# Stage 1 of a triangle update: four chunks batched singly, and a shift row asked for one step after its store

## Chip, cores, metric

The kernel runs on one core of one Trainium2 chip. The metric is the device time of one execution in microseconds; a median of three runs is given. A profile comes from one further execution of the same program, which has its own time.

## What is computed

The input x is 384 x 384 positions of 128 channels, all fp32. Two layers follow each other:

```
# layer 0
z     = layernorm(x)
left  = (z @ Wl + bl) * sigmoid(z @ Wlg + blg)
right = (z @ Wr + br) * sigmoid(z @ Wrg + brg)
core  = einsum('bikh,bjkh->bijh', left, right)
x     = x + sigmoid(x @ Wg + bg) * (layernorm(core) @ Wout + bout)
# layer 1
left  = x @ (W_left + W_eq) + biases
out   = left * sum_j(x @ W_right + b_right) * sigmoid(x @ W_gate + b_gate)
x     = layernorm(out @ W_out + b_out + x)
```

## The kernel before, in words

**Three stages.** Stage 1 (to about 1000 us) makes `left` and `right` and stores them in DRAM as `lr_d`. Stage 2 (to about 1700 us) makes `core` for one channel h after another, 18 fp32 matmul passes each. Stage 3 does the rest row by row. The change touches stage 1 alone.

**Stage 1's unit.** A chunk n is 8 x 128 positions of x; there are 144. A chunk is worked off in two steps, so step k = 2n + q, with q = 0 or 1; a step is two halves of two 128x512 matmuls (`back`, L362: matmul L372 into a PSUM tile `pr`, of which there are three; sigmoid on ScalarE L383; gating on VectorE L385, which writes the tile `lr`). Each fp32 matmul is recorded as two passes, so a step is 8 passes.

**The layer norm.** For z, the matmul needs x minus its mean, with the reciprocal root of the variance applied afterwards as a scale. VectorE takes the statistics of each position from `xt` (L263). Statistics are finished in batches of chunks: `powers` (L265, VectorE, L275 to L279) makes moments, `power` (L282, GpSimd, L286) raises to the power -0.5, once for 8 columns, at most once a step, and `centres` (L292, VectorE, L303 and L304) makes the shift `nd`. `begin` (L451) starts a batch when its statistics are there and fewer than two batches are under way; it is called once a step, as is `centres`.

**How the shift reaches the data.** The first 8 chunks are loaded with positions in partitions, shifted there (L320) and transposed on TensorE (L335, by `front`). From chunk 8 on, the chunk is loaded a second time with channels in partitions (`load_columns`, L129, tile `xc`, four buffers). Its shift must then lie along the free dimension, in all partitions alike. So `store_nd` (L346) writes the batch's `nd` to DRAM, in pieces of 16 bytes; `load_shift` (L136, DMA on L139) reads one row of 512 values into partition 0 of a tile `bc` (four buffers), for each step one row; and `shift` (L314) broadcasts it over the partitions on GpSimd (L323) and subtracts it from the columns (L324). From step 10 on, step k of the program holds the shift for step k + 2.

**What sets the order.** The order on every engine is that of the program. All DMAs of the stage are issued by SyncE in order, so a DMA whose wait isn't fulfilled holds up all that follow. In each step the loop at L459 issues, in this order: a store of shifts that has become due (L348), the columns of chunk n + 4 (L134, in the second step of a chunk), rows of shifts (L139), chunks for the statistics (L127), one slice of 1 MB of a finished `lr` tile (L357, `store_slice`). A tile `lr` holds 8 chunks; its 8 slices go out in the steps after its last chunk, so for the first tile in steps 15 to 22.

**The batches.** Chunks 0 to 9 are batches of one, then come (10, 11), (12, 13) and so on in pairs. **When a row is asked for:** L501 looks at the first row that is still wanted. It is asked for when it is at most 6 steps ahead, and its store lies in an earlier step; if it is more than 3 steps ahead, the store must lie at least two steps back.

Of the kernel before, what the change touches and what calls it, by code (L numbers as in the profile page):

```python
# [19 lines left out]
def triangle_then_gated_row_kernel(ctx: ExitStack, tc: tile.TileContext, a: dict, out: bass.AP):  # L20
# [35 lines left out]
    def seq(ins):  # L56

        return tc.keep_in_program_order(ins)
# [4 lines left out]
    def load(dst, src, queue=nc.sync):  # L63
        seq(queue.dma_start(out=dst, in_=src))
# [12 lines left out]
    chunks = [(kb, ig, c) for kb in range(NB) for ig in range(NG) for c in range(G // XR)]  # L77
    kept = {(NB - 1, ig): None for ig in range(NG - KEEP, NG)}
    end2 = ctx.enter_context(ExitStack())
    with ExitStack() as ctx2:  # L80
# [16 lines left out]
        with tc.tile_pool(name="p1w", bufs=5, side="right") as wp, \  # L97
# [6 lines left out]
            NQ = XR // 4  # L104
            AHEAD, LEAD = 4, 15
            FETCH = 6
# [1 line left out]
            loaded, normed = {}, {}  # L108
            lr, full = {}, []
            batches, at = [(n, n + 1) for n in range(PLAIN)], PLAIN  # L110
            for size in [1, 1] + [2] * len(chunks):
                if at < len(chunks):
                    batches.append((at, min(at + size, len(chunks))))
                    at = batches[-1][1]
# [167 lines left out]
            def power():  # L282

                own, lo, hi, span = pows.pop(0)
                sd, rs = (t[:, lo:hi] for t in terms[own][2:])
                seq(nc.gpsimd.tensor_tensor(rs, sd, mhalf[:, :hi - lo], ALU.pow))  # L286
                if hi == span[1]:
                    means.append((own, span))
                    if 0 < own[0] < PLAIN:
                        centres(1)  # L290
# [16 lines left out]
            centred, stored = [], {}  # L307
# [6 lines left out]
            def shift(n, q, rows=slice(0, 4)):  # L314


                s = slice(4 * q + rows.start, 4 * q + rows.stop)
                if n < PLAIN:
                    nd = nds[n, n + 1][:, s].unsqueeze(2).to_broadcast([P, rows.stop - rows.start, C])
                    seq(nc.gpsimd.tensor_tensor(loaded[n][:, s], loaded[n][:, s], nd, ALU.subtract))  # L320
                else:
                    z, t = columns[n][:, q].rearrange("c k i -> c (k i)"), shifts.pop((n, q))
                    seq(nc.gpsimd.partition_broadcast(t, t[0:1]))  # L323
                    seq(nc.gpsimd.tensor_tensor(z, z, t, ALU.subtract))  # L324

            def front(n, q, rows=slice(0, 4)):

                if n < PLAIN:  # L330
                    s = slice(4 * q + rows.start, 4 * q + rows.stop)
                    columns[n] = loaded[n]
                    pt = tps.tile([P, 4, P], F32, tag="pt", name="pt")
                    for r in range(s.start, s.stop):
                        seq(nc.tensor.transpose(pt[:, r - s.start, :], loaded[n][:, r, :], ident))  # L335
                    seq(nc.scalar.copy(columns[n][:, s], pt[:, :s.stop - s.start]))
# [25 lines left out]
            def back(n, q, half, between=None):  # L362


                kb, ig, c = chunks[n]
                if c == 0 and q == 0 and half == 0:
                    lr[kb, ig] = lrp.tile([P, H, G, 2], F32, tag="lr", name="lr")
                t = lr[kb, ig]
                pr = pps.tile([P, 2, 4 * H], F32, tag="pr", name="pr")
                for r in range(2):  # L370
                    i = 2 * half + r
                    seq(nc.tensor.matmul(  # L372
                        pr[:, r, :], lhsT=columns[n][:, 4 * q + i, :] if n < PLAIN else columns[n][:, q, :, i],
                        rhs=wz, start=True, stop=True,
                    ))
                    if r == 0 and between:
                        between()
                r0 = 4 * q + 2 * half
                own, c0 = normed[n]
                rs = [terms[own][3][:, c0 + r:c0 + r + 1] for r in range(r0, r0 + 2)]  # L380
                sg = [wp.tile([P, 2 * H], F32, tag="sg", name="sg") for _ in range(2)]
                for r in range(2):
                    seq(nc.scalar.activation(sg[r], pr[:, r, 2 * H:], AF.Sigmoid, scale=rs[r]))  # L383
                for r in range(2):
                    seq(nc.vector.scalar_tensor_tensor(  # L385
                        t[:, :, c * XR + r0 + r, :],
                        pr[:, r, :2 * H].rearrange("k (h s) -> k h s", s=2),
                        rs[r],
                        sg[r].rearrange("k (h s) -> k h s", s=2),
                        ALU.mult, ALU.mult,  # L390
                    ))
                if c == G // XR - 1 and q == NQ - 1 and half == 1:
                    if (kb, ig) in kept:
                        kept[kb, ig] = t
                    else:
                        full.extend((kb, ig, hs, t) for hs in range(0, H, HS))
# [40 lines left out]
            want = [i for i, (n, q) in enumerate(steps) if n >= PLAIN]  # L437

            def goal(k):

                if k < 0:
                    return 2 * AHEAD
                return 2 * (k + 1) + min(2 * LEAD, 10 + (10 * k + 6) // 7 if k < 8 else 20 + 2 * (k - 7) // 3)

            for n in range(PLAIN, len(chunks)):
                k = 2 + (n - PLAIN) // 2
# [4 lines left out]
            def begin(k):  # L451

                while waiting and 2 * NQ * waiting[0][1] <= given and (k == 0 or free()):
                    own = waiting.pop(0)
                    powers(own, 0, XR * (own[1] - own[0]))
                    if k > 0:
                        break

            for k, (n, q) in enumerate(steps):  # L459
                early = len(means)  # L460
                for _ in range(min(len(pows), 1)):
                    power()
                early = 0 if k in (6, 7, 8) else early if k > 8 else len(means)
                if k > 0:
                    more = 4 if k in (6, len(steps) - 6) else 1
                    while shifted < min(len(steps), k + 2 + more):
                        shift(*steps[shifted])
                        shifted += 1
                    if more > 1:
                        lib = library_config.all_libraries[10] if k == 6 else library_config.standard  # L470
                        seq(nc.gpsimd.load_library(lib))
                for half in range(2):
                    if k == 0:

                        back(n, q, half, (lambda: front(*steps[1])) if half else None)
                        if half == 0:
                            centres(len(means))
                            shift(*steps[2])
                            shifted = 3
                    else:  # L480
                        back(n, q, half)
                        if half == 0:
                            centres(early)
                        if half == 0 and k + 1 < len(steps):
                            front(*steps[k + 1])
                    if half == 0 and k > 0:
                        begin(k)
                    stats_to((goal(k - 1) + goal(k)) // 2 if half == 0 else goal(k))
                if k == 0:
                    begin(k)  # L490
                    power()
                if q == NQ - 1:
                    del loaded[n], normed[n], columns[n]
                while centred:
                    own = centred.pop(0)
                    if own[0] >= PLAIN:
                        store_nd(own)
                        stored.update({m: k for m in range(*own)})
                if q == NQ - 1:
                    load_columns(n + 4)  # L500
                while want and want[0] <= k + FETCH and stored.get(want[0] // NQ, k) < k - (want[0] > k + 3):  # L501
                    load_shift(*steps[want.pop(0)])
                assert not want or want[0] > k + 3
                for m in fetch.get(k, []):
                    load_chunk(m)
                store_slice()
                if k == 4:
                    for t, src in later:
                        load(t, src)
                if k == 20:  # L510
                    m2 = late_weights()
                if k == 24:
                    late_products(m2)
                if k == len(steps) - 2 * G // 4 + 16:
                    assert not full
                    for h in range(2):
                        load_h(h)
# [465 lines left out]
```

## Time and profile before

| | |
|---|---|
| median of 3 runs | 3162.54 us (3160.98 to 3163.11) |
| the profiled execution: its time | 3165.75 us |
| its span, first to last instruction | 3163.6 us |
| TensorE busy | 3138.1 us (99%) |
| VectorE, ScalarE, GpSimd busy | 2471.1, 1805.8, 2396.2 us |
| L372, stage 1's matmul on `xc` | 2176 passes, 937.6 us |
| L357, L127, L134: one transfer | 1024, 512, 512 KB |
| L348, store of a pair or of one chunk; L139, one row | 8 or 4 KB; 2 KB |

A timeline line is: start in us, duration, engine, line, operation, tiles, count; in brackets the idle time before it and what ended that. `PE` is TensorE, `DVE` VectorE, `ACT` ScalarE, `POOL` GpSimd, `SPq` SyncE's issue of a DMA (not its transfer). A line of a window gives, after its length, the busy time of TensorE, its weight loads, VectorE, ScalarE and GpSimd, then the granted TensorE clock, the share of the DMA engines, and GB/s. When a DMA lands is read from the updates of its semaphore, which the trace also holds.

### The profile page before, as it was taken

How to read it: one execution, taken by the hardware profiler on the slowest of the kernel's cores; microseconds unless marked ns; L12 is line 12 of the kernel's file. 1: busy time of each engine (PE TensorE's matmuls, PEld its weight loads, DVE VectorE, ACT ScalarE, POOL GpSimd, SP SyncE). 2: the span in 40 equal slices, each digit the busy share in tenths (PEclk: the TensorE clock that was granted, in tenths of full speed). 3: DMA queues.
4: the chain of work that ended last, by engine and by line, in shares of the span. 5: the costliest groups of instructions: out<-in, count | busy, mean ns of one | idle time of the engine just before them, and what ended most of it. 6: DMA issues, size and time to landing. Idle time of an engine off the chain costs nothing.

```text
span 3163.6 us, 44516 instructions
## 1 busy us (share of the span) xinstructions
PE 3138.1 (99%) x11306; PEld 2133.0 (67%) x11306; DVE 2471.1 (78%) x7395; ACT 1805.8 (57%) x3755; POOL 2396.2 (76%) x3066
## 2 busy tenths in 40 slices
PE   9999999999999999999999999999999999999998
PEld 4677777777776666666666566677777777777776
DVE  8788888888886555555555788888888888888998
ACT  4444444444444334334343577677777777777776
POOL 6788888888886665666666587788888888888887
PEclk9999999999999999999999999999999999999999
DMA  4887878888883999999999865666666666666562
GB/s 163 290 327 276 341 281 323 292 318 309 295 326 96 281 283 284 284 281 284 282 282 284 287 239 198 225 223 220 220 220 220 220 220 220 220 220 220 210 211 109
DMA packets 509070, 797.42 MB, mean 252 GB/s; under 512 B 56657, under 2 KB 419537, under 8 KB 492434
## 3 DMA queue, kind: packets, MB, share of 16 engines
q1 hardware_dynamic: 507520, 792.61, 73.8%
q8 instruction: 94, 1.54, 0.2%
q10 hardware_dynamic: 1234, 1.77, 0.2%
q14 instruction: 158, 1.29, 0.1%
q0 software_dynamic: 64, 0.20, 0.0%
HBM read 508.14 MB, written 286.36 MB: 251 GB/s over the span
## 4 chain that ended last, share of the span: by engine, by line
PE 97%; DVE 1%; DMA 0%; issue 0%; POOL 0%; ACT 0%; SPq 0%; POOLq 0%; DVEq 0%; ACTq 0%
PE pr L372 30%; PE pc L611 23%; PE py L781 8%; PE pr L752 8%; PE pg L769 8%; PE pl L770 8%; PE pg L721 8%; PE py L782 4%; DMA core_d<-ct 0%; DVE lr L385 0%; POOL rs L286 0%; PE pq L729 0%; DVE st L263 0%; PE pt L335 0%; DMA stage<-in_x_nat_dram 0%
## 5 line engine op out<-in xcount | busy, mean ns | idle before, releaser
L372 PE MATMUL pr<-wz,xc 128*128 128x512 f32 x2176 | 937.6, 594 | 5.7 <-POOL xc L324 4.6
L372 PEld LDWEIGHTS pr<-wz,xc 128*128 128x128 f32 x2176 | 670.6, 308 | 272.0 <-issue 5.4
L383 ACT ACTIVATE sg<-pr,rs 128x256 f32<-128x256 f32 x1152 | 482.7, 470 | 517.6 <-ACT sg L383 354.6
L611 PE MATMUL pc<-rr,lrh 128*128 128x384 f32 x2304 | 743.3, 486 | 0.4 <-DVE lr L385 0.4
L611 PEld LDWEIGHTS pc<-rr,lrh 128*128 128x128 f32 x2304 | 452.0, 196 | 291.8 <-issue 1.1
L385 DVE SCALAR_TENSOR_TENSOR lr<-pr,rs,sg 128x256 f32<-128x256 f32 x1152 | 502.6, 478 | 174.8 <-ACT sg L383 169.4
L816 ACT ACTIVATE py<-py,nm,rs 128x128 f32<-128x128 f32 x1149 | 491.9, 429 | 158.7 <-DVE u L774 80.1
L781 PEld LDWEIGHTS py<-wo,u 128*128 128x128 f32 x2304 | 376.6, 191 | 97.5
L622 DVE TENSOR_TENSOR csum<-csum,ct 128x1152 f32<-128x1152 f32 x127 | 175.4, 1381 | 333.7 <-ACT ct L620 333.7
L781 PE MATMUL py<-wo,u 128*128 128x128 f32 x2304 | 402.0, 275 | 0.0
L620 ACT COPY ct<-pc 128x1152 f32<-128x1152 f32 x127 | 142.2, 1119 | 445.3 <-PE pc L611 439.7
L743 POOL TENSOR_TENSOR cs<-ct,rt 128x384 f32<-128x384 f32 x380 | 378.7, 998 | 8.3 <-PE pg L769 4.2
L851 POOL TENSOR_TENSOR yt<-yt,lnb 128x384 f32<-128x384 f32 x380 | 379.7, 1001 | 2.9 <-DVE yt L845 2.6
L324 POOL TENSOR_TENSOR xc<-xc,bc 128x512 f32<-128x512 f32 x272 | 345.8, 1271 | 24.0
L286 POOL TENSOR_TENSOR rs<-nd,mhalf 128x8 f32<-128x8 f32 (+1 forms) x145 | 236.3, 1630 | 145.7 <-ACT sg L383 112.7
L796 DVE BATCH_NORM_STATS2 st<-py 128x6 f32<-128x128 f32 x1152 | 266.4, 287 | 88.7 <-PE py L782 86.7
L592 POOL COPY rr<-lrh 128x768 f32<-128x768 f32 x128 | 196.4, 1534 | 161.0 <-DMA lrh<-lr_d 150.3
L782 PE MATMUL py<-ident,x1T 128*128 128x128 f32 x1152 | 314.0, 273 | 0.0
L752 PE MATMUL pr<-cs,wc 128*128 128x384 f32 x768 | 313.5, 490 | 0.0
L721 PE MATMUL pg<-xt,mat_L_conv_Wg 128*128 128x384 f32 x768 | 310.7, 487 | 2.0 <-ACT ct L635 2.0
L769 PE MATMUL pg<-x1T,mat_L_conv_W_gate 128*128 128x384 f32 x768 | 310.7, 486 | 0.9 <-ACT g L772 0.9
L770 PE MATMUL pl<-x1T,mat_L_conv_W_left 128*128 128x384 f32 x768 | 310.5, 486 | 0.0
(124 smaller groups left out, 4297.0 us busy)
## 6 DMA issues: line engine op xcount, KB each, us to landing
lr_d<-lr SPq DMA_DIRECT2D x128, 1024.0 KB
lrh<-lr_d SPq DMA_DIRECT2D x128, 640.0 KB
xt<-in_x_row_dram SPq DMA_DIRECT2D x96, 768.0 KB
ct<-core_d SPq DMA_DIRECT2D x95, 768.0 KB
rt<-rstd_d SPq DMA_DIRECT2D x95, 768.0 KB
out_dram<-yt SPq DMA_DIRECT2D x94, 768.0 KB
core_d<-ct SPq DMA_DIRECT2D x125, 576.0 KB
xt<-in_x_nat_dram SPq DMA_DIRECT2D x136, 512.0 KB
```

The source lines that it names most:

```text
L372: seq(nc.tensor.matmul(pr[:, r, :], lhsT=columns[n][:, 4 * q + i, :] if n < PLAIN else columns[n][:, q, :, i], rhs=wz, start=True, stop=Tr ...
L383: seq(nc.scalar.activation(sg[r], pr[:, r, 2 * H:], AF.Sigmoid, scale=rs[r]))
L385: seq(nc.vector.scalar_tensor_tensor(t[:, :, c * XR + r0 + r, :], pr[:, r, :2 * H].rearrange("k (h s) -> k h s", s=2), rs[r], sg[r].rearra ...
L611: seq(nc.tensor.matmul(banks[ib], lhsT=t[:, kb, ib * P:(ib + 1) * P, 0], rhs=rr[:, kb], start=(kb == 0), stop=(kb == NB - 1),))
L721: seq(nc.tensor.matmul(pg[:, :N], lhsT=wg0, rhs=r["xT"], start=True, stop=True))
L752: seq(nc.tensor.matmul(pr[:, :N], lhsT=wc, rhs=r["cs"], start=True, stop=True))
L769: seq(nc.tensor.matmul(pg2[:, :N], lhsT=wgate, rhs=r["x1T"], start=True, stop=True))
L770: seq(nc.tensor.matmul(pl[:, :N], lhsT=wleft, rhs=r["x1T"], start=True, stop=True))
L781: seq(nc.tensor.matmul(py[:, s], lhsT=r["u"][:, s], rhs=r["wo"], start=True, stop=False))
L782: seq(nc.tensor.matmul(py[:, s], lhsT=r["x1T"][:, s], rhs=ident, start=False, stop=True, is_transpose=True))
L816: seq(nc.scalar.activation(py[:, s], py[:, s], AF.Identity, bias=bias, scale=scale))
L851: seq(engine.tensor_tensor(yt, yt, lnbb, ALU.add))
```

## The change

Two lines. The list of batch sizes after the first 8 chunks begins with six ones in place of two, so chunks 10, 11, 12 and 13 are batches of their own, and pairs begin with (14, 15). And a row may be asked for in the step after the step of its store, however far ahead it is wanted.

```diff
-            for size in [1, 1] + [2] * len(chunks):
+            for size in [1] * 6 + [2] * len(chunks):
...
-                while want and want[0] <= k + FETCH and stored.get(want[0] // NQ, k) < k - (want[0] > k + 3):
+                while want and want[0] <= k + FETCH and stored.get(want[0] // NQ, k) < k:
                     load_shift(*steps[want.pop(0)])
```

The order of the program around it becomes, step by step (S: store of a batch's shifts, R: row asked for):

| step | before | after |
|---|---|---|
| 11 | | R 8,0 and 8,1 |
| 12 | S 9; R 8,0 and 8,1 | S 9 |
| 13 | | S 10; R 9,0 and 9,1 |
| 14 | R 9,0 and 9,1 | R 10,0 |
| 15 | | S 11; R 10,1 |
| 16 | S 10-11 | S 12; R 11,0 |
| 17 | R 10,0 | R 11,1 |
| 18 | R 10,1, 11,0 and 11,1 | S 13; R 12,0 |
| 19 | S 12-13 | R 12,1 |
| 20 | | R 13,0 |
| 21 | R 12,0, 12,1, 13,0 and 13,1 | R 13,1 |
| 22 | S 14-15 | S 14-15 |
| 23 | | R 14,0 and 14,1 |
| 24 | R 14,0, 14,1 and 15,0 | R 15,0 |
| 26, 27 | in 27: R 16,0 and 16,1 | in 26: R 16,0; in 27: R 16,1 |

From step 28 on both are alike. On VectorE the moments of 10-11 (step 13) and 12-13 (step 16) become those of 10, 11, 12 and 13 (steps 11, 13, 14, 16), their `centres` those of steps 13, 15, 16 and 18 in place of 16 and 19. On GpSimd the powers of steps 14, 15, 17 and 18 become those of steps 12, 14, 15 and 17. Instructions of other kinds are neither added nor moved.

## Prediction

> **What bounds the kernel now.** I read the page's chain of waits first, then TensorE's waits, then the stretch in which it waits, engine by engine. The unit below is the step k = (n, q) of stage 1: half a chunk n, 8 matmul passes (each fp32 matmul is recorded as two). T(k) is the time at which its first pass starts; "row (n,q)" is the 2 KB shift row that L139 fetches for it.
>
> ```profile
> span 3163.6 us, 44516 instructions
> ...
> PE 97%; DVE 1%; DMA 0%; issue 0%; POOL 0%; ACT 0%; SPq 0%; POOLq 0%; DVEq 0%; ACTq 0%
> ```
> TensorE's own work is 97% of the chain, so only time in which it stands still or runs slowly can be won. Its waits over the whole run are short; the first two lines are:
>
> ```profile
> PE pr L372 <- POOL xc L324: 4.6, 1, 4.6
> PE pr L372 <- ACT sg L383: 2.0, 2, 1.1
> ```
> One wait of 4.6 us on GpSimd's subtraction. The timeline places it, and the windows give the clock around it:
>
> ```profile
> 73.86 13.90 PE L372 MATMUL pr<-wz,xc 128*128 128x512 f32 x32
> 92.37 16.60 PE L372 MATMUL pr<-wz,xc 128*128 128x512 f32 x32 [4.62 <-POOL xc L324]
> 110.07 3.79 PE L372 MATMUL pr<-wz,xc 128*128 128x512 f32 x8 [1.10 <-ACT sg L383]
> ```
> ```profile
> 87.75:92.37 4.62, 0.01 (x1) 0.00 (x0) 3.04 (x16) 0.84 (x2) 2.05 (x2) 0.82 1.03 427
> 92.37:99.57 7.20, 7.20 (x11) 3.72 (x12) 1.27 (x4) 1.68 (x4) 6.66 (x6) 0.64 1.04 369
> 99.57:110.07 10.50, 9.41 (x22) 6.17 (x22) 10.40 (x33) 5.03 (x12) 6.16 (x6) 1.00 0.88 317
> ```
> 32 passes are four steps, k = 16 to 19, in 13.76 us: 3.44 us a step. The next four took 16.60, because after the standstill the granted clock is 0.64 (third number from the end) and 11 passes need 7.20 us. Then 1.10 us more are lost. Unhindered, T(24) would be 73.86 + 8 x 3.44 = 101.38; it is 110.07. **8.7 us** are at stake: 4.7 standstill, 2.9 slow clock, 1.1 second wait. From 114.9 us on TensorE doesn't pause again in this stage.
>
> Who is late? GpSimd, for a row, and SyncE's queue says why:
>
> ```profile
> 82.47 1.63 POOL L286 TENSOR_TENSOR rs<-nd,mhalf 128x8 f32<-128x8 f32 x1
> 90.18 0.80 POOL L323 PARTITION_BROADCAST bc<-bc  x1 [6.08 <-DMA bc<-nd_d]
> 91.06 1.26 POOL L324 TENSOR_TENSOR xc<-xc,bc 128x512 f32<-128x512 f32 x1
> ```
> ```profile
> 77.90 1.42 SPq L348 DMA_DIRECT2D nd_d<-nd  x1
> 80.63 0.33 SPq L127 DMA_DIRECT2D xt<-in_x_nat_dram  x1
> 81.01 0.45 SPq L357 DMA_DIRECT2D lr_d<-lr  x1
> 84.96 0.24 SPq L139 DMA_DIRECT2D bc<-nd_d  x1
> ```
> Shifts of chunks 10 and 11 are stored together at 77.90 (step 16). By the trace's completion events the store lands at 84.94, behind a 512 KB load and the first 1 MB slice of lr_d; row (10,0) is asked for at 84.96 and lands at 90.09, behind two more large transfers. Two trips through a full queue; TensorE starts 2.28 us after the row has landed (broadcast, subtraction, hand-over).
>
> **The skill.** "TensorE: Matmul & The Clock Gate", What's actually happening: an idle window of about 3.4 us puts the clock to half. The trace agrees: 4.62 us idle gave 0.64 over the next 7.2 us, 1.10 us idle left 1.00. "DMA: Bandwidth & Descriptors", Queues, rings and completion order: every engine consumes a ring's descriptors in order. It agrees: a 2 KB row took 1.3 us at 63.3 us, 5.1 us at 84.96. "SBUF — State Buffer", SBUF: two separate sides: a VectorE operation with two SBUF inputs and a GpSimd operation block each other. It agrees: L232 on 128x1 took 1.25 us under an L324, L279 1.23 us under another, 0.19 us elsewhere.
>
> **The change, part by part.** Replaying the step loop by hand gives each queue's order; from step 28 on both programs are the same.
>
> 1. *Row (10,0).* Chunk 10 is a batch of its own: moments in step 11, power in 12, store in 13 (about 66.8 us), row asked for in step 14, once its buffer is free (four rows, so after the shift of (8,0), which ends at 71.1). The DMAs are nearly idle then; it lands near 73. GpSimd reaches this shift at about 82.3 and ends it at 84.4; TensorE wants it at T(20) = 87.6. The 4.62 us wait and its slow clock go.
>
> 2. *VectorE and GpSimd.* Four single batches replace two pairs: 14 more VectorE instructions, 2 x (0.7 + 0.3) = 2 us in steps 11 to 18, where it waits 0.45 to 0.9 us for ScalarE in most half steps. One batch's moments (step 14, about 70.2) fall under the L324 of 69.8 to 71.1: up to 0.9 us; the next L385 would be 0.65 late against over 0.8 of slack in PSUM buffers. Cost 0. GpSimd does as many powers; the one put before the shift of (7,0) ends that shift near 62, needed at 64.4. Cost 0. Without these covers: up to 2 us.
>
> 3. *SyncE.* Two more stores (0.38 us of issue each), and the load of columns 11 moves behind a store, from 70.4 to about 74.8, wanted at 90: hidden, but its 0.5 MB now start the congested stretch; I add 0.3 us to what lands later. Rows (11,0) to (13,1) land between about 85 and 107; the tightest, (13,0), stored at 84.8, landed at 92.7, asked for at once, lands near 103.8 against a limit of 107.
>
> 4. *VectorE after step 20.* L227 to L234 still fall there (1.7 us in before) and 22's moments follow. This is what ended in the 1.10 us wait at T(24), with two operations stretched by GpSimd. GpSimd is ahead now and idle at step 22's moments. Bounds 0 and 1.1; I take 0.4.
>
> 5. *What is late next: row (14,0).* TensorE now runs 8.7 us earlier, but the eight lr_d slices (8 MB, steps 15 to 22) take the DMAs as long as before. In before the queue was never empty from 77 to 105; slice 6 landed at 104.89, columns 14 at 106.15. That stays. Between 84.77 and 106.15, 8 MB landed: 2.67 us per MB (2.4 for the quickest slices). Behind columns 14 come chunk 22 (0.5 MB), slice 7, the store of (14,15), chunk 23, slice 8, columns 15. An issue also waits for the eighth before it (eight semaphores in turn), so that store goes out at about 100. It lands 1.5 x 2.67 + 0.1 after 106.15: 110.3. Only then is row (14,0) asked for, now in step 23, and it stands behind 2 MB that are already queued: 110.3 + 5.1 = 115.4 (+0.3 of item 3 and -0.3 as a row rides on one ring and often lands ahead of the load before it). T(28) unhindered is 101.38 + 15.13 (as before's steps 24 to 28, L240 to L243 included) + 0.4 = 116.9. With the row it is 115.4 + 2.28 = 117.7: **0.8 us** of wait. Row (14,1) follows behind a power: its shift ends 1.64 + 2.13 = 3.8 us after the first, a step is 3.44: 0.3 more. Bounds: landing at 113.8 costs nothing, at 117.5 it costs 3.3.
>
> Sum: 8.7 - 0.4 - 0.8 - 0.3 = **7.2 us** less. All that follows is TensorE-bound and shifts as a whole. The profiled run took 3165.75 us (span 3163.6): 3158.6. Median shown 3162.54: **3155.3**.
>
> **Rivals.**
> - *No new wait*: the queue drains at 2.4 us per MB and row (14,0) lands by 114. For: slices 2, 3, 5 and 6 came at 2.4 to 2.5. Against: slices 1 and 4 took 4.2 and 3.5. Gain 8.7 - 0.4 = 8.3: 3154.2.
> - *The wait at step 28 is large*: the row lands at 117.5 and more. T(29) is then 117.5 + 6.0 = 123.5 instead of before's 128.6: gain 5.1, and if the standstill passes the idle window, 2.9 less. For: store-to-row trips of 7 us each way occur throughout 77 to 106. 3157.4 to 3160.3, middle 3158.5.
> - *Slower*: the same place, worse. If both trips of row (14,0) take 11.3 us, the longest latency in the stretch (slice 6), it lands at 100.1 + 22.6 = 122.7; T(29) = 122.7 + 6.0 + 2.9 for the clock = 131.6, against 128.6: 3.0 slower, 3165.5. It decides from a landing of 119.8 on. Against: a trip is 11 us only with 4 MB ahead, and the last slices have 2 MB.
> - *The change doesn't reach the wait*: row (10,0) still late. It would need 11 us in an empty queue. 3162.5.
>
> **How the numbers follow.** My forecast 0.53, no new wait 0.21, large wait 0.20, slower 0.04, not reached 0.02. 0.2% is 6.3 us, about what a measurement here can tell from no change: below 3156.2 lie the second case and some 0.44 of the first, so faster 0.65, same 0.31, slower 0.04. The range 3153.6 to 3159.0 holds the first two and most of the third; about 0.17 is left out, mostly above.
>
> **What would show it.** After: no wait on L324 near 88 us and clock 1.00 there; T(24) at 101.4 to 102.5; the 1.10 us wait smaller; a short wait of TensorE on L324 near 117 us, with GpSimd waiting for a row just before; from 121 us on the same picture as before's from 128.6. Wrong if GpSimd waits for another row, (13,0) first, if TensorE waits for VectorE in steps 12 to 19, or if the slow clock shows up again.

## The result, and the profile after

| | before | after |
|---|---|---|
| median of 17 runs each | 3162.64 us (3159.77 to 3164.42) | 3155.39 us (3154.33 to 3157.71) |
| the profiled execution: its time, its span | 3165.75, 3163.6 us | 3154.78, 3152.9 us |

The ratio is 0.9978 with an interval of 0.9971 to 0.9984: 7.25 us less by the medians, 5.1 to 9.2 by the interval. The forecast was 7.2 us less, 3155.3. The two profiled executions are 11 us apart, which is more than the medians; why is taken up below.

The page of the changed kernel, its span and its group of L372 (busy us, mean ns, idle before):

```profile
span 3152.9 us, 44536 instructions
...
L372 PE MATMUL pr<-wz,xc 128*128 128x512 f32 x2176 | 935.1, 592 | 0.0
```
The same 2176 passes take 935.1 us in place of 937.6: the slow clock is gone, and with it the idle time ahead of the group. The lines of TensorE's waits (us in total, times, longest) for other engines that fall in stage 1:

```profile
PE pt L335 <- POOL stage L320: 1.8, 2, 1.2
PE p L169 <- DVE avg L152: 1.0, 1, 1.0
PE pr L372 <- ACT sg L383: 0.9, 1, 0.9
```
No wait on L324 is listed any more, and of the two on ScalarE one is left, from the start of the stage. The timeline of TensorE, where neighbours without a visible pause are one line:

```profile
73.76 31.17 PE L372 MATMUL pr<-wz,xc 128*128 128x512 f32 x72
...
105.80 239.55 PE L372 MATMUL pr<-wz,xc 128*128 128x512 f32 x556
```
72 passes are the nine steps 16 to 24 in one piece, where before had 32, then 4.62 us of nothing, 32, 1.10 us, and 8. The windows at the times at which before stood still and ran slowly:

```profile
87.60:92.37 4.77, 4.77 (x13) 3.44 (x12) 4.70 (x20) 2.52 (x6) 3.27 (x3) 1.00 1.03 417
92.37:99.57 7.20, 7.20 (x19) 5.15 (x18) 6.55 (x27) 3.36 (x8) 6.11 (x6) 1.00 1.03 421
99.57:110.07 10.50, 10.50 (x33) 7.67 (x32) 8.79 (x36) 4.58 (x12) 9.38 (x8) 1.00 1.03 404
```
Clock 1.00 throughout, 19 passes in the 7.20 us that held 11. The DMA share (1.03 in all three) is no lower than it was (1.03, 1.04, 0.88): the queue is at least as full as before, only row (10,0) no longer stands in it. SyncE's queue and GpSimd show its way:

```profile
66.60 0.37 SPq L348 DMA_DIRECT2D nd_d<-nd  x1
...
71.21 0.22 SPq L139 DMA_DIRECT2D bc<-nd_d  x1
...
100.29 1.25 SPq L348 DMA_DIRECT2D nd_d<-nd  x1
...
111.57 0.87 SPq L139 DMA_DIRECT2D bc<-nd_d  x3
```
```profile
82.62 0.80 POOL L323 PARTITION_BROADCAST bc<-bc  x1
83.50 1.28 POOL L324 TENSOR_TENSOR xc<-xc,bc 128x512 f32<-128x512 f32 x1
...
114.13 0.80 POOL L323 PARTITION_BROADCAST bc<-bc  x1 [1.55 <-DMA bc<-nd_d]
115.02 1.27 POOL L324 TENSOR_TENSOR xc<-xc,bc 128x512 f32<-128x512 f32 x1
```
The store of chunk 10 is issued at 66.60, row (10,0) at 71.21, and it lands at 73.17; GpSimd takes it at 82.62 without a wait. The next late row is (14,0): store issued at 100.29, landed at 111.50, row asked for at 111.57, landed at 114.05, GpSimd 1.55 us without work. Its subtraction ends at 116.29 and T(28) is 116.34.

Slips of some tenths don't break a line of the timeline; they are read from the starts of the single passes, normally 0.43 us apart. Steps 28 and 29 take 7.39 us from start to start in place of 6.87: 0.52 us lost. Up to there only 0.10 are lost, within step 24.

### The profile page after: what moved, and what is told of

It is laid out like the page before. It is cut to its first block, busy times and chain, and to the rows that moved or that the text cites. A ratio compares the mean times of both kernels' runs of the same rounds, so it can differ in the third digit from the quotient of the medians.

```text
span 3152.9 us, 44536 instructions
## 1 busy us (share of the span) xinstructions
PE 3135.5 (99%) x11306; PEld 2132.8 (68%) x11306; DVE 2473.6 (78%) x7409; ACT 1808.5 (57%) x3755; POOL 2392.9 (76%) x3066
## 4 chain that ended last, share of the span: by engine, by line
PE 98%; DVE 1%; ACT 0%; issue 0%; DMA 0%; POOL 0%; POOLq 0%; DVEq 0%; ACTq 0%
PE pr L372 31%; PE pc L611 23%; PE py L781 8%; PE pr L752 8%; PE pg L769 8%; PE pl L770 8%; PE pg L721 8%; PE py L782 4%; DMA core_d<-ct 0%; PE pt L335 0%; PE pq L729 0%; ACT py L816 0%; PE pb L740 0%; POOL rs L286 0%; DVE m L547 0%
## 5 line engine op out<-in xcount | busy, mean ns | idle before, releaser
L372 PE MATMUL pr<-wz,xc 128*128 128x512 f32 x2176 | 935.1, 592 | 0.0
L372 PEld LDWEIGHTS pr<-wz,xc 128*128 128x128 f32 x2176 | 670.5, 308 | 263.9 <-POOL xc L324 1.2
L324 POOL TENSOR_TENSOR xc<-xc,bc 128x512 f32<-128x512 f32 x272 | 345.8, 1271 | 24.0
L769 PE MATMUL pg<-x1T,mat_L_conv_W_gate 128*128 128x384 f32 x768 | 310.7, 486 | 0.9 <-ACT g L772 0.9
L721 PE MATMUL pg<-xt,mat_L_conv_Wg 128*128 128x384 f32 x768 | 310.7, 487 | 0.3 <-ACT ct L635 0.2
```

The lines of the kernel that those rows point to most:

```text
L372: seq(nc.tensor.matmul(pr[:, r, :], lhsT=columns[n][:, 4 * q + i, :] if n < PLAIN else columns[n][:, q, :, i], rhs=wz, start=True, stop=Tr ...
L721: seq(nc.tensor.matmul(pg[:, :N], lhsT=wg0, rhs=r["xT"], start=True, stop=True))
L769: seq(nc.tensor.matmul(pg2[:, :N], lhsT=wgate, rhs=r["x1T"], start=True, stop=True))
```

## The experiments

Two theories stand against each other. *Mine*: before's loss is one chain, row (10,0) behind a full queue, then a standstill, then a slow clock and a second wait as its aftermath; the batches end it, and row (14,0) gives a little back. *Rivals*: the rule does it, not the batches; the slow clock or the late weights are losses of their own, which go without touching the row; the queue isn't what makes the row late.

Since executions of one kernel differ by more than some of the effects, the table gives the medians (13 to 21 runs, beside 41 or 56 of the kernel before on the same chip), and from the one trace of each T(24) and T(32) counted from T(16). Steps without any loss give 27.5 and 56.2. The ratios are the measurement's own, not the quotient of the two medians. None of these kernels leaves out any of the computation.

| kernel | median | before beside it | ratio, interval | T(24) | T(32) |
|---|---|---|---|---|---|
| before, first trace | | | | 36.21 | 65.11 |
| before_again | 3161.90 | 3162.56 | 1.0000, 0.9992 to 1.0009 | 32.30 | 61.75 |
| before_third | 3162.73 | 3162.56 | 1.0001, 0.9993 to 1.0009 | 33.73 | 63.34 |
| after, first trace | | | | 27.47 | 56.84 |
| after_again | 3155.67 | 3162.41 | 0.9979, 0.9971 to 0.9987 | 27.47 | 57.14 |
| rule_alone | 3161.20 | 3162.56 | 0.9996, 0.9988 to 1.0004 | 35.06 | 63.76 |
| batches_alone | 3156.61 | 3162.56 | 0.9983, 0.9976 to 0.9989 | 27.47 | 58.58 |
| batches_again | 3156.18 | 3162.56 | 0.9982, 0.9973 to 0.9990 | 27.46 | 57.14 |
| singles_to_15 | 3157.11 | 3162.56 | 0.9983, 0.9976 to 0.9989 | 29.59 | 58.49 |
| pe_kept_busy | 3162.82 | 3162.41 | 1.0002, 0.9994 to 1.0010 | 33.06 | 63.68 |
| slices_later | 3158.24 | 3162.56 | 0.9987, 0.9981 to 0.9994 | 29.14 | 58.04 |
| slices_pause | 3155.38 | 3162.41 | 0.9977, 0.9969 to 0.9986 | 27.47 | 56.24 |

weights_later moves work out of these steps and is told below.

**Both parts by themselves.** The rule alone:

```diff
-                while want and want[0] <= k + FETCH and stored.get(want[0] // NQ, k) < k - (want[0] > k + 3):
+                while want and want[0] <= k + FETCH and stored.get(want[0] // NQ, k) < k:
```

> Only the second line of the change: a row may be asked for one step after its store; batches as before. Theory (the batches of one do the work, the rule next to nothing): row (10,0) is asked for in step 17 as before, since its store is in step 16, so the 4.6 us standstill stays; 0 to -1 us, near 3162. Rival (the earlier requests do a good part): at least -3 us, with the wait before step 24 gone, since rows of 12 are asked for in step 20 in place of 21.

```profile
92.30 20.23 PE L372 MATMUL pr<-wz,xc 128*128 128x512 f32 x40 [4.53 <-POOL xc L324]
```
The standstill is whole, the clock after it 0.61 over 7.2 us. The store of chunks 10 and 11 still goes out in step 16 and lands at 85.01; the row is asked for at 85.02, so for row (10,0) there is nothing that the rule could move forward. It does move the rows of chunk 12: row (12,0) is asked for at 98.30, right after its store has landed (98.22), and lands at 102.83, against 102.54 and 106.34 in before; this trace has no second wait at step 24. The median is 1.4 us below before's, but the interval holds 1: by itself the rule is worth nothing that these runs resolve. The batches alone:

```diff
-            for size in [1, 1] + [2] * len(chunks):
+            for size in [1] * 6 + [2] * len(chunks):
```

> Only the first line: chunks 10 to 13 in batches of one, the rule as before. Theory: row (10,0) is asked for in step 15 near 75 us and lands before 81, rows of 11 in step 17 and land by 90; both in time, so the whole gain is here: -6.5 to -8 us against before, within 1 us of the changed kernel. Row (14,0) stands in the text of step 24, but nothing is queued between on SyncE, so it is asked for at the same time. Rival (both lines are needed): a standstill of 1 us or more on a row of chunk 11 near 91 us or of 14 near 116, and half of the gain.

TensorE and GpSimd in this kernel:

```profile
106.02 10.67 PE L372 MATMUL pr<-wz,xc 128*128 128x512 f32 x24
118.27 27.31 PE L372 MATMUL pr<-wz,xc 128*128 128x512 f32 x62 [1.58 <-POOL xc L324]
```
```profile
116.06 0.80 POOL L323 PARTITION_BROADCAST bc<-bc  x1 [3.26 <-DMA bc<-nd_d]
```
The standstill near 88 us is gone, so it was the batches. Row (14,0) lands at 115.97 here, 1.92 us later than in the changed kernel, and TensorE waits 1.58 us at step 28. Whether the missing rule does that was looked at with the same kernel once more.

> The first line of the change alone, once more. The first time it stood 1.2 us above the changed kernel, and its trace had row (14,0) landing at 116.0 us (114.0 and 114.4 with both lines), though SyncE's order is the same from step 18 on. Theory (the landing of that row varies from one execution to the next): now within 0.7 us of 3155.5, or the row at 114 to 115 us in the trace. Rival (the rule takes that microsecond): the row lands at 115.5 or later again and the time is 1 us above the changed kernel again.

This time the row landed at 114.95 and step 28 was 0.32 us late. In after_again, which is the changed kernel once more, it landed at 114.44, with the same 0.3 us:

> The changed kernel, unchanged, timed and profiled once more. The trace of the kernel before, taken twice, had standstills of 4.78 and 2.85 us at step 20, with and without a slow clock, and step 25 at 114.7 and 111.1 us; so the changed kernel's own spread is wanted too. Theory (it has lost the part that varies): step 25 starts within 0.3 us of 105.8 and no slow clock; row (14,0) lands between 114 and 116 us and costs TensorE 0.3 to 2.3 us at steps 28 and 29. -7.2 us against before, within 1 us. Rival (the batches-alone kernel, 1.2 us slower, shows that the rule matters): here row (14,0) lands by 114.2 again, and the wait is below 0.6 us.

So the landing moves by about a microsecond from one execution to the next with either rule. The medians, of different chips in part, leave 0.5 to 1.2 us to the rule, within the intervals: that the rule adds something to the batches isn't shown.

**Is the full queue what makes the row late?** Before, with the first slices of `lr_d` put off by six steps:

```diff
-                store_slice()
+                if k >= 21:
+                    store_slice()
```

> The kernel before, pairs and rule as they are, with the first lr tile's eight slices sent in steps 21 to 28 in place of 15 to 22. It tests the cause of the standstill: is it the pairing (the store comes too late in the program) or the full queue (two trips behind 1 MB slices)? Theory (the full queue): the store of step 16 lands near 81 us, row (10,0) near 85, and TensorE doesn't wait at step 20; rows of 12 and 14 are in time as well; step 25 starts near 105.8: -6.5 to -8.5 us, as much as the change, with the batches untouched. Rival (the pairing): a standstill of 2 us or more at step 20 stays, or one appears at steps 24 to 36 when the slices come later: less than -4 us.

TensorE, then VectorE, then GpSimd:

```profile
87.93 14.40 PE L372 MATMUL pr<-wz,xc 128*128 128x512 f32 x32 [0.26 <-POOL xc L324]
102.92 3.79 PE L372 MATMUL pr<-wz,xc 128*128 128x512 f32 x8 [0.59 <-ACT sg L383]
...
137.42 2.08 PE L372 MATMUL pr<-wz,xc 128*128 128x512 f32 x4 [0.28 <-DVE lr L385]
139.95 5.51 PE L372 MATMUL pr<-wz,xc 128*128 128x512 f32 x12 [0.45 <-DVE lr L385]
```
```profile
99.85 1.16 DVE L276 TENSOR_TENSOR st<-st 128x16 f32<-128x16 f32 x1
```
```profile
99.70 1.27 POOL L324 TENSOR_TENSOR xc<-xc,bc 128x512 f32<-128x512 f32 x1
```
With batches and rule as in before, the store now lands in 3.2 us in place of 7.1, the row is asked for at 81.44 and lands at 85.64, and the standstill shrinks from 4.62 to 0.26 us: the queue is the cause. Most of what is won is the store's trip; the row's own takes 4.20 us in place of 5.13. The expected gain was missed, 4.3 us by the medians: VectorE is late three times after it, near 102, 137 and 139.5 us (the last two cost 1.5 us more, beyond T(32) in the table). At 99.85 its L276, 0.19 us elsewhere, lies under an L324 for 1.16 us, and step 24 waits. That wait comes with a standstill of only 0.26 us ahead of it.

**The slow clock by itself.** Before, with four fp32 matmuls of constants into an unused tile after step 19, so that TensorE has work while it waits for the row:

```diff
+                if k == 19:
+                    fill = tps.tile([P, 4, P], F32, tag="pt", name="fill")
+                    for _ in range(4):
+                        seq(nc.tensor.matmul(
+                            fill.rearrange("p a b -> p (a b)"), lhsT=avg,
+                            rhs=avg.unsqueeze(1).to_broadcast([P, 4, P]), start=True, stop=True,
+                        ))
```

> The kernel before, with four matmuls of a constant into an unused PSUM tile after step 19: they take 3.4 us of the standstill, so that TensorE never stands idle for long; nothing of the result uses them. Theory (half clock after a long standstill is a cost of its own, 2.9 us where it happens): the granted clock stays 1.00, and steps 20 to 23 take 13.8 us in every execution; the row is as late as before. The median falls by 1 to 3 us, as part of the executions of before have the slow clock (one of two traces). Rival (the slow steps after the standstill are late rows, not the clock): no change, and the passes after it are as sparse as before.

TensorE, the window from its second stop on, and GpSimd:

```profile
87.45 3.60 PE L513 MATMUL fill<-avg 128*128 128x512 f32 x8
90.88 13.90 PE L372 MATMUL pr<-wz,xc 128*128 128x512 f32 x32
106.77 5.52 PE L372 MATMUL pr<-wz,xc 128*128 128x512 f32 x8 [1.99 <-POOL xc L324]
```
```profile
106.77:112.10 5.33, 5.33 (x8) 2.68 (x9) 1.51 (x6) 0.84 (x2) 5.24 (x5) 0.68 0.91 271
```
```profile
104.56 0.79 POOL L323 PARTITION_BROADCAST bc<-bc  x1 [4.21 <-DMA bc<-nd_d]
```
Steps 20 to 23 run at full clock, 32 passes in 13.90 us. But step 24 then waits 1.99 us for row (12,0), for which GpSimd has waited 4.21 us, and four passes run at half clock after that. The median gains nothing. What is won at step 20 is waited for at step 24, since the rows of chunk 12 come when the queue lets them come.

**Two more traces of before** say what the slow clock and the second wait do when the standstill is shorter.

> The kernel before, unchanged, timed and profiled once more, to see what repeats. Ratio 1.000. Theory (the standstill at step 20 is built into the order of the program): the new trace shows it again, 4.5 to 5 us on L324 near 88 us, the granted clock below 0.7 after it, and a second wait of about 1.1 us at step 24; step 25 starts at 114 to 115.5 us. Rival (the profiled execution was an unlucky one, 3.1 us above the median): the standstill is 2 us shorter or the clock stays at 1.00. The 2.0 us wait of TensorE on ScalarE at the seam of stages 2 and 3 either repeats (then it belongs to the kernel) or not (then it explains most of the 3.1 us).

> The kernel before, profiled a third time, since the size of the gain hangs on what before loses in a usual execution. So far step 25 started at 114.7 (execution of 3165.8 us) and at 111.1 us (3160.2 us). Theory (what varies is the landing of row (10,0), the slow clock after it, and a late row of 12 or a late VectorE at step 24): the three pieces again, step 25 between 110 and 115 us, and the execution's time fits: about 1 us more for each us that step 25 starts later. Rival (the spread comes from the seam of stages 2 and 3): step 25 near one of the old values, and time and step 25 don't go together.

The first of them:

```profile
90.69 14.12 PE L372 MATMUL pr<-wz,xc 128*128 128x512 f32 x32 [2.68 <-POOL xc L324]
106.41 3.82 PE L372 MATMUL pr<-wz,xc 128*128 128x512 f32 x8 [1.59 <-POOL xc L324]
```
The second:

```profile
91.37 15.82 PE L372 MATMUL pr<-wz,xc 128*128 128x512 f32 x32 [3.58 <-POOL xc L324]
107.62 3.82 PE L372 MATMUL pr<-wz,xc 128*128 128x512 f32 x8 [0.43 <-POOL xc L324]
```
Row (10,0) landed at 90.09, 88.41 and 89.08 in the three traces, the standstill was 4.62, 2.68 and 3.58 us, the clock over the next 7.2 us 0.64, 1.00 and 0.76. Where the standstill and the clock cost least, the second wait cost most, 1.59 us; in these two traces it is a wait for a row of chunk 12. Why the clock differed so much is taken up in the last section. Against the 56.2 without loss the three lose 8.9, 5.5 and 7.1 us up to T(32), 7.2 on average.

**The late weights.** Before, with L227 to L234 at step 40 and the products L240 to L243 at step 44:

```diff
-                if k == 20:
+                if k == 40:
...
-                if k == 24:
+                if k == 44:
```

> The kernel before with the weight preparation moved from steps 20 and 24 to steps 40 and 44. It tests the cause that the prediction gave for the second wait (1.1 to 1.8 us at step 24). Theory: VectorE's four operations of step 20 (1.7 us) are what makes it late at step 24; without them the wait there is below 0.4 us in a trace with the long standstill: -1 us. Rival: the wait is an aftermath of the standstill (late rows of 12 and GpSimd colliding with VectorE) and stays at 1 us or more: 0 us.

TensorE and VectorE:

```profile
90.75 16.96 PE L372 MATMUL pr<-wz,xc 128*128 128x512 f32 x32 [2.93 <-POOL xc L324]
108.45 36.92 PE L372 MATMUL pr<-wz,xc 128*128 128x512 f32 x84 [0.74 <-ACT sg L383]
```
```profile
104.92 0.58 DVE L276 TENSOR_TENSOR st<-st 128x16 f32<-128x16 f32 x1
...
105.76 1.23 DVE L279 TENSOR_TENSOR nd<-nd,st 128x16 f32<-128x16 f32 x1
```
The second wait is still there, 0.74 us on ScalarE as before's 1.10, and the ratio is 1.0002 (0.9994 to 1.0010; median 3162.92 beside 3162.41). Without the weights, L276 and L279 are the operations that VectorE is held up by, the second under the L324 of 105.68 to 106.95. That the weights had no part at all in before's 1.10 us can't be read from one trace of each.

**More of the same.** The change, with chunks 14 and 15 single too, so that row (14,0) isn't late:

```diff
-            for size in [1] * 6 + [2] * len(chunks):
+            for size in [1] * 8 + [2] * len(chunks):
```

> The changed kernel with chunks 14 and 15 as batches of one too. It tests the step of the prediction that row (14,0) is late next. Theory: row (14,0) is then asked for in step 22 after a store of step 19, lands before 110 us, and the slips of TensorE at steps 28 and 29 (0.23 and 0.31 us in the trace of the changed kernel) go: -0.5 us against the changed kernel, 3154.9. Rival (the slips have another cause, or the next row is late in its place): no difference, or slips at step 32.

TensorE, VectorE and GpSimd:

```profile
84.84 12.44 PE L372 MATMUL pr<-wz,xc 128*128 128x512 f32 x28 [0.41 <-DVE lr L385]
97.46 2.08 PE L372 MATMUL pr<-wz,xc 128*128 128x512 f32 x4 [0.17 <-DVE nd L303]
99.92 7.44 PE L372 MATMUL pr<-wz,xc 128*128 128x512 f32 x16 [0.38 <-DVE lr L385]
```
```profile
81.63 1.27 DVE L275 TENSOR_TENSOR mv<-st 128x16 f32<-128x16 f32 x1
```
```profile
81.58 1.27 POOL L324 TENSOR_TENSOR xc<-xc,bc 128x512 f32<-128x512 f32 x1
```
The row is in time (asked for at 100.31, landed at 107.84), but the kernel isn't faster than the change: its median is 1.4 to 1.7 us above the two of the change, and its T(32) as much later, though the intervals of the ratios overlap. TensorE now waits for VectorE three times, and T(24) is 2.1 us late. The new moments of 81.63 coincide with an L324 of GpSimd for their whole length. The expectation of a further gain was wrong.

**Row (14,0) by another way.** The change, with slices 7 and 8 of the first tile moved from steps 21 and 22 to 23 and 24, behind the store and its row:

```diff
-                store_slice()
+                if k not in (21, 22):
+                    store_slice()
```

> The changed kernel with slices 7 and 8 of the first lr tile held back from steps 21 and 22 to 23 and 24, so that they stand behind the store of (14,15) and row (14,0) on SyncE and not ahead of them. It tests the next bound that the prediction named. Theory (row (14,0) is late because 2 MB of slices stand ahead of its store and of itself): it lands before 112 us, and steps 28 and 29 start without a slip: -0.5 to -1.5 us against the changed kernel, 3154 to 3155. Rival (the next row or the columns behind the slices are late in their place): a slip of the same size at steps 30 to 34, no gain.

TensorE, SyncE's queue and GpSimd:

```profile
106.16 39.42 PE L372 MATMUL pr<-wz,xc 128*128 128x512 f32 x91
```
```profile
99.50 0.90 SPq L348 DMA_DIRECT2D nd_d<-nd  x1
...
108.13 0.58 SPq L139 DMA_DIRECT2D bc<-nd_d  x2
```
```profile
112.92 0.80 POOL L323 PARTITION_BROADCAST bc<-bc  x1
```
The store lands at 108.08, the row at 109.40, 1.27 us after it was asked for. GpSimd doesn't wait for it, and steps 28 and 29 lose nothing: T(32) is at the 56.2 without loss, 0.6 and 0.9 us ahead of the two traces of the change. By the medians it is 0.3 us faster than after_again on the same chip, which these runs don't resolve. In the medians it is level with the change; in its trace it is the one kernel that loses nothing up to T(32).

## Why the prediction was right, and where it wasn't

**At stake, 8.7 us.** The place and the chain were right: the row, the store ahead of it, the queue. In the profiled pair T(24) came 8.84 us earlier. But the 8.7 us belong to one execution, 3.1 us above the median, and to the costliest of three traces; on average the three lose 7.2 us up to T(32). In one reading the prediction fell short: ahead of row (10,0) stood three transfers of 2 MB together, not two. They landed at 86.19, 88.67 and 89.90, the row at 90.09.

**Item 1, row (10,0).** Right: landed at 73.17 ("near 73"), subtraction at an end by 84.78 (84.4), T(20) 87.50 (87.6), clock 1.00.

**Item 2, cost 0 on VectorE and GpSimd.** Right, and the cover is what the prediction named. L275 of step 14 took 1.12 us at 70.09, under the L324 that ends at 71.19 (0.17 to 0.19 us elsewhere), and no step from 16 to 19 is late. That is the block between VectorE and GpSimd that the prediction took from the Trainium skill ("SBUF — State Buffer", SBUF: two separate sides), and the trace agrees again. singles_to_15 shows what it costs where the cover ends: the same operation, 1.27 us at 81.63, makes step 19 late by 0.77 us.

**Item 3, SyncE.** No loss, as forecast: columns 11 issued at 74.92 (74.8), landed at 80.35; row (13,0) landed at 100.99, earlier than the 103.8 of the forecast.

**Item 4, 0.4 us after step 20.** The number was too high and its cause wrong. The weights fall after step 20 as forecast, at 93.24, but beside no L324: L232 takes 0.15 us, 1.25 in before. Step 24 loses 0.10. And, as far as one trace tells, the weights hadn't made before's second wait: without them it stays, 0.74 us (weights_later). What the prediction named beside them is what is left: statistics on VectorE that meet GpSimd's subtractions (weights_later). In two of three traces of before it is a row of chunk 12 instead. Either goes with the change. That both are an aftermath of the standstill is not shown: rule_alone has the whole standstill and the slow clock without a second wait, since its rows of chunk 12 come earlier, and slices_later has the wait with hardly a standstill. VectorE's half of it is a matter of what it happens to meet, the rows' half one of the queue.

**Item 5, row (14,0).** The place, the mechanism and the step were right, the size half: 0.52 us lost in place of 1.1. Row (14,1)'s 0.3, behind a power, came as forecast: its subtraction ends at 120.02, T(29) is 120.08, and step 28 took 3.74 us. Of the 0.8 for row (14,0) 0.2 are left. (The item's bounds of 113.8 and 117.5 leave out the 0.4 of item 4; with its own T(28) of 116.9 a landing at 117.5 costs 2.9 and, with row (14,1), 3.2.) The first trip ended 1.2 us later than forecast, at 111.50 (110.3). The term that failed is the second: 2.5 us in place of 5.1, though the 2 MB had been issued ahead of it. Slice 8, issued eight microseconds earlier, landed from 111.95 to 114.78, columns 15 from 112.98 to 116.02; the row passed both with 114.05. Had it come after columns 15, it would have taken 4.5 us. The Trainium skill, "DMA: Bandwidth & Descriptors", Why a DMA increments its semaphore by 16 and not by 1, says that a transfer uses up to 16 engines and each in use adds one when its part has landed, while the rest is added at once. The trace agrees: slice 8 has 16 updates spread over 2.8 us, the row one at 111.97 and one at 114.05. A row rides on one ring and is through as soon as that one is; the forecast had allowed 0.3 us for this. It wasn't the only such row: (13,0) landed 1.8 us ahead of the 1 MB slice issued just before it (100.99 and 102.78). That this ring ran ahead is what the spread suggests, and which ring a slice's updates belong to wasn't looked at.

**The sum.** Two sizes were off, 8.7 at stake and 1.5 given back, and the errors cancel in part. The pair of traces gave more than 7.2: 8.4 us by the end of stage 1, and 2.3 more between there and stage 3 (to the first L769: 757.5 us in before, 755.2 after). The second isn't the change: the same stretch took 755.4 and 756.3 us in before's other traces, and 757.1 in the change's other. It goes with TensorE's wait for a copy on ScalarE (L721 on L635) at the seam of stages 2 and 3, which was 2.0, 0.2 and 0.8 us in before's three traces and 0.2 and 1.6 in the change's two. In means the gain to T(32) is 63.4 - 57.0 = 6.4 us, in medians 7.25. What the runs support is thus 7.2 at stake with 0.6 to 0.9 given back, rather than 8.7 less 1.5, in a measurement whose interval is 5.1 to 9.2 us. The direction and the mechanism were reasoned rightly; that the median came within 0.1 us of the forecast is luck.

**The rivals.** No new wait: near, but row (14,0) does cost something; slices_pause shows the kernel without it. The large wait: batches_alone came closest, 2.3 us with a landing at 115.97, and no half clock after 1.58 us of idle. Slower needs a landing past 119.8; the latest seen was 115.97. Its first trip did come, 11.2 us for the store; its second didn't. Not reached: excluded by the trace. The four traces with the batches of the change have row (14,0) landing at 114.05 to 115.97 and lose 0.6 to 2.3 us up to T(32): the cost at step 28 varies with the execution.

## What to carry to other kernels

A small result that goes out to DRAM and comes back pays the queue twice, so move both trips ahead of the bulk transfers, or the bulk behind them; a rule that allows an earlier request moves nothing forward while the store is late. Where the same data are small, single batches buy time until their operations on VectorE meet GpSimd's: two more of them brought nothing here, and the medians stand 1.4 to 1.7 us higher. And before a sum is made against one profiled execution, ask how far that execution stands from the median: 8.7 us at stake were 5 to 9 from trace to trace.

## What the runs showed of the hardware that was not expected

The half clock doesn't follow from the length of the idle time alone. The Trainium skill, "TensorE: Matmul & The Clock Gate", What's actually happening, puts it after an idle window of about 3.4 us, and says that the window runs freely. Idle times and the clock that followed: 4.62 us, 0.64; 4.53, 0.61; 3.58, 0.76; 2.93, 0.59; 2.68, 1.00; 1.99 (pe_kept_busy), 0.68 over 5.3 us, with full speed for the first 1.5 us after the restart and half speed for the next four passes; 1.58 (batches_alone), 1.00. So the measurement has half clock after idle times well below 3.4 us, and of 2.68 and 1.99 us the shorter one was the dearer. What decides can be worked out from the traces. All changes of the granted clock in them lie a whole number of periods of 3.413 us apart, the length that the page gives its window: the first stretch at full clock lasts 85.33 us in before, before_third, rule_alone and weights_later (25 periods) and 102.40 in pe_kept_busy (30), the half clock in stage 1 3.41 or 6.83 us (1 or 2). Cut into these periods, weights_later, before_again and pe_kept_busy look like this (the first busy time is TensorE's, the clock is the third number from the end):

```profile
86.47:89.88 3.41, 1.35 (x4) 0.52 (x2) 3.24 (x15) 1.40 (x4) 1.25 (x2) 1.00 1.02 423
89.88:93.30 3.42, 2.55 (x3) 1.22 (x4) 1.53 (x6) 0.00 (x0) 2.94 (x4) 0.50 1.03 426
```
```profile
85.71:89.12 3.41, 2.30 (x6) 1.23 (x4) 3.28 (x13) 1.68 (x4) 0.62 (x1) 1.00 1.02 416
89.12:92.54 3.42, 1.85 (x4) 1.47 (x5) 3.39 (x12) 0.00 (x0) 2.85 (x4) 1.00 1.01 415
92.54:95.95 3.41, 3.41 (x9) 2.46 (x8) 1.84 (x7) 1.68 (x4) 3.32 (x4) 1.00 1.22 379
```
```profile
104.83:108.25 3.42, 1.48 (x3) 1.16 (x4) 2.18 (x8) 0.84 (x2) 3.33 (x3) 1.00 0.94 348
108.25:111.66 3.41, 3.41 (x5) 1.33 (x4) 1.25 (x4) 0.84 (x2) 3.32 (x4) 0.50 0.91 252
```
In weights_later 2.06 of the 2.93 us of idle time fell into one period and left TensorE 1.35 us of work in it; the next period ran at half clock. In before_again the 2.68 us fell across two periods and left 2.30 and 1.85, and the clock stayed. In pe_kept_busy nearly all of the 1.99 us fell into one period and left 1.48: half clock. In all thirteen traces, the ends of the kernels included, a period at full clock with at most 1.48 us of work was followed by half clock, and one with at least 1.66 us (near the end of rule_alone) never was. Once at half, the clock stayed there after periods with 1.71 to 2.55 us of work (before, rule_alone, weights_later) and was full again after one that was busy throughout. The first rise to full clock lies between 3.90 and 7.20 us after the span's start, so where the borders of the periods fall on a standstill changes from execution to execution: how much slow clock before has is chance. This is read from the traces afterwards; no run set the position of the periods.

Where VectorE's small operations meet GpSimd's L324, they can take nearly its whole length. In singles_to_15 L275 took 1.27 us in place of 0.19, L304 1.18 in place of 0.17, and L234, which has one tensor as input, 1.30 (at 95.22, under the L324 of 95.17) in place of 0.22. What it costs is decided by the half step that it falls into: L275's 1.27 us cost 0.77 us in singles_to_15, its 1.12 us nothing in the changed kernel.
